# A spectral convolution block in float32: from three merged streams of steps per batch to one fixed period over all batches

## The chip, the cores and the metric

The kernel runs on one core of a Trainium2 chip. The metric is the device time of one execution in microseconds (us), from three runs.

## The reference

The input `x` has 4 batches of 256 x 256 positions with 64 channels, float32. Two layers follow each other. Cut to what is computed:

```python
# layer 0
h  = pw(ln(x, g1, b1), w_te, b_te)                  # 64 -> 128 channels
F  = fft2(h, axes=(1, 2))
fc = gelu(pw(concat(real(F), imag(F)), w_fc, b_fc)) # 256 -> 256
sp = real(ifft2(fc[..., :128] + 1j * fc[..., 128:]))
x1 = x + pw(sp, w_tp, b_tp)                         # 128 -> 64
h2 = pw(ln(x1, g2, b2), w_fe, b_fe)                 # 64 -> 128
d  = gelu(depthwise_conv3x3(h2, w_dw) + b_dw)
x  = x1 + pw(d, w_fp, b_fp)                         # 128 -> 64
# layer 1, along the first image axis, 256 long
trend = moving_average(x, 25)
ys    = einsum('bmnc,cmk->bknc', rfft(x - trend)[:, :128], w_real + 1j * w_imag)
out   = trend + irfft(ys, n=256)
```

## The kernel before

All transforms are matrix products with tables, in float32. Layer 0 is cut into three streams, each a Python generator for one batch that yields after every step.

- `forward_h`, 32 chunks of 8 columns per batch: load `xt`, statistics (`measure`: a square on ScalarE, sums on VectorE), scaling on GpSimd (`norm`), sums of halves on VectorE (`halves`, L341, L343), the transform along the first axis (`transform`, L353, result `ps_y`), copy to `yt`, store to `y_d` in HBM.
- `spectral`, 65 pairs of rows of frequencies per batch, two or three pairs to a group: load `yb`, `transform_w` (L434 with the whole array, L438 and L439 with halves of its columns, result `ps_x`, copied to `xs`), `mix` (L453, halves of its rows, four banks `ps_p`), sums on VectorE (L470), GELU on ScalarE (`activate`, L476), `fold` (L483, one half on VectorE, one on GpSimd), `project` (L508, halves of the columns, `ps_z` copied to `zs`), `turn` (L521, transposes), and once per group `back_w` (L537) with a store to `u_d` in HBM.
- `convolution`, 32 chunks of 8 columns per batch: load `uc` and `x1`; `back_h` (L625, halves of the rows, then three sums on VectorE, L633 and L637); `measure` (square `sq_c`, L294); `norm`; `to_channels` (L657, transposes, copied to `tt`); `row_sums` (L673 to L678); four products of the 3x3 convolution in a form with three row sums per pair of rows: each product is two matmuls with the whole array (`wc_main`, L692) and four with halves of its rows (`wc_half`, L705) into two banks `ps_h`. Products 1 and 2 are `conv_first` (a copy on ScalarE, L724, and four sums on VectorE, L726 and L727), products 0 and 3 `conv_rest` (L733), then `edges` (L745), GELU (`activate`, L750), `finish` in two halves (L756 with halves of the columns, `ps_f` copied to `fs`, L764) and `store` in two halves (transposes L774 of `fs`, sums on VectorE L784, store to `x2_d` in HBM).

So a matmul uses the array as a whole, as two halves of its rows, or as two halves of its columns, and the instructions of one function can be of more than one of these kinds. All results go through one pool of eight PSUM banks. Each bank is reused when the last reader of its former tile is done.

The order of TensorE, VectorE, ScalarE and GpSimd is that in which the Python code issues the instructions (`manual_schedule`); each engine keeps it. SyncE, which issues all DMAs, is ordered by the tile framework. Before, `spaced` gives every step of a generator a place on a common axis, `all_batches` chains the four batches of a stream, and `merge` always advances the stream whose next place is lowest:

```python
at = {
    all_batches(spectral, mixing, 5 * 69, -1.0, -0.08): -1.0,
    all_batches(forward_h, fwd, 4 * 33, -2.05, -1.1): -2.05,
}
...
at[all_batches(convolution, conv, 11 * 36, 0.0, 1.0)] = 0.0
```

The steps of the streams are thus interleaved one by one, by place alone. `convolution` has 36 rounds of 11 steps for 32 chunks: at the start and at the end of each batch its pipeline of five chunks fills and drains. A fourth generator, `matrices`, works out the matrices of layer 1 beside the first batch's `forward_h` (L865, L866, L875). At the end `layer1` (L948) multiplies all batches by them.

Of the kernel before, what the change touches and what calls it, by code (L numbers as in the profile page):

```python
# [2 lines left out]

# [8 lines left out]
F32 = mybir.dt.float32  # L12
# [6 lines left out]
P = 128  # L19
N = 256  # L20
# [88 lines left out]
def conv_seq_kernel(ctx: ExitStack, tc: tile.TileContext, a: dict, tables: bass.AP, out: bass.AP):  # L109
# [7 lines left out]
    spill = ctx.enter_context(tc.tile_pool(name="spill", bufs=2, space=DRAM))  # L117
# [188 lines left out]

    y_ds, u_ds = {}, {}

    def forward_h(b, pool):

        WH = 4
        y_d = spill.tile([P, N, 2, C], F32, tag="y_d", name=f"y_d_{b}")
        y_ds[b] = y_d
# [3 lines left out]
        def load(q):  # L319

            xt = pool.tile([P, 2, 2, WH, C], F32, tag="xt", name=f"xt_{b}_{q}", bufs=3)
            for hf in range(2):
                w0 = hf * P + q * WH
                nc.sync.dma_start(
                    xt[:, :, hf],
                    x[b, :, w0 : w0 + WH, :].rearrange("(t p) w c -> p t w c", p=P),
                )
            chunks[q] = xt

        def measure(q):  # L330
            var[q] = statistics(pool, flat(chunks[q]), f"{b}_{q}")

        def norm(q):
            xt = flat(chunks[q])
            scale(pool, xt, xt, var.pop(q), f"{b}_{q}")

        def halves(q):
            xt = chunks[q]
            xb = pool.tile([P, 2, 2, WH, C], F32, tag="xb", name=f"xb_{b}_{q}", bufs=1)
            for i, op in enumerate((ALU.add, ALU.subtract)):  # L340
                nc.vector.tensor_tensor(xb[:, :, i], xt[:, :, 0], xt[:, :, 1], op)  # L341
            for i, op in enumerate((ALU.add, ALU.subtract)):
                nc.vector.tensor_tensor(xt[:, i], xb[:, 0], xb[:, 1], op)  # L343

        def transform(q):
            n = f"{b}_{q}"
            xt = chunks.pop(q)
            yt = pool.tile([P, 2, WH, 2, C], F32, tag="yt", name=f"yt_{n}")
            for m in range(2):
                ps = bank(f"ps_y_{n}_{m}")  # L350
# [12 lines left out]
            for par in range(2):  # L363
                w0 = par * P + q * WH
                nc.sync.dma_start(y_d[:, w0 : w0 + WH], yt[:, par])

        NCH = P // WH
        load(0)
        for q in range(NCH + 1):
            if q + 1 < NCH:  # L370
                load(q + 1)
            if q < NCH:
                measure(q)
            yield
            if q >= 1:
                halves(q - 1)
            yield
            if q < NCH:
                norm(q)
            yield  # L380
            if q >= 1:
                transform(q - 1)
            yield

    def spectral(b, pool):

        y_d = y_ds.pop(b)
        u_d = spill.tile([P, N, 2, C], F32, tag="u_d", name=f"u_d_{b}")
        u_ds[b] = u_d
        KG, ZS = 4, 1  # L390
        groups, per_group = {}, {}

        def load_group(g):
            n = f"{b}_{g}"
            yb = pool.tile([P, 2, KG, 2 * C], F32, tag="yb", name=f"yb_{n}")
            for t in range(2):
                nc.sync.dma_start(
                    yb[:, t],
                    y_d[g * KG : (g + 1) * KG, t * P : (t + 1) * P].rearrange(
# [3 lines left out]
            groups[g] = yb  # L403

        def begin(g):
            n = f"{b}_{g}"
            yb = groups[g]
            blocks = [(yb, k) for k in range(KG)]
            if g == 0:

                yr = pool.tile([P, 2, 2, 2 * C], F32, tag="yr", name=f"yr_{n}", bufs=1)
# [6 lines left out]
            zt = pool.tile([P, 2, 2, KG, C], F32, tag="zt", name=f"zt_{n}")  # L418
            groups[g] = zt
            per_group[g] = [blocks[i : i + 2] for i in range(0, len(blocks), 2)]  # L420

        def transform_w(pr):
            xs = pool.tile([P, 2, N], F32, tag="xs", name=f"xs_{pr['n']}")
            pr["xs"] = xs
            nb = len(pr["blocks"])
            ps = bank(f"ps_x_{pr['n']}")
            todo = [
# [3 lines left out]
            ]  # L431

            for i, (dst, y, t) in enumerate(todo):
                nc.tensor.matmul(dst, y, cw[:, t, :], start=i == 0, stop=False)  # L434

            for i, (dst, y, t) in enumerate(todo):
# [3 lines left out]
            nc.scalar.copy(xs.rearrange("p j n -> p (j n)")[:, : nb * N], ps[:, : nb * N])  # L440
# [87 lines left out]
        def back_w(g):  # L528
            zt = groups.pop(g)
            ut = pool.tile([P, 2, KG, 2, C], F32, tag="ut", name=f"ut_{b}_{g}")  # L530

            pss = []
            for t in range(2):
                ps = bank(f"ps_u_{b}_{g}_{t}")
# [15 lines left out]
            for wt in range(2):  # L550
                nc.sync.dma_start(
                    u_d[g * KG : (g + 1) * KG, wt * P : (wt + 1) * P].rearrange(
# [5 lines left out]
        prs = []  # L558
        NG = P // KG
        for g in range(NG):  # L560
            slot = 0
            count = KG // 2 + (g == 0)
            for i in range(count):
                prs.append({"g": g, "i": i, "n": f"{b}_{g}_{i}", "special": g == 0 and i == 0})
                prs[-1]["last"] = i == count - 1
                prs[-1]["slot"] = slot
                slot += 1 if prs[-1]["special"] else 2
        load_group(0)
        begin(0)
        for i in range(len(prs) + 4):  # L570
            if i < len(prs):
                pr = prs[i]
                pr["blocks"] = per_group[pr["g"]][pr["i"]]
                transform_w(pr)
                if pr["last"] and pr["g"] + 1 < NG:
                    load_group(pr["g"] + 1)
            if 0 <= i - 2 < len(prs):
                fold(prs[i - 2])
            yield
            if 0 <= i - 4 < len(prs) and prs[i - 4]["last"]:  # L580
                back_w(prs[i - 4]["g"])
            yield
            if 0 <= i - 1 < len(prs):
                mix(prs[i - 1])
            yield
            if 0 <= i - 3 < len(prs):
                turn(prs[i - 3])
            yield
            if 0 <= i - 2 < len(prs):
                project(prs[i - 2])  # L590
            if 0 <= i - 1 < len(prs):
                activate(prs[i - 1])
            if i < len(prs) and prs[i]["last"] and prs[i]["g"] + 1 < NG:
                begin(prs[i]["g"] + 1)
            yield

    def convolution(b, pool):

        u_d = u_ds.pop(b)
# [4 lines left out]
        x1s, ucs, var, xns, ts, ends, stores = {}, {}, {}, {}, {}, {}, {}  # L604
        rows = lambda t: t.rearrange("p t w c -> p (t w) c")

        def load(q):
            n = f"c_{b}_{q}"
            uc = pool.tile([P, W, 2, C], F32, tag="uc", name=f"uc_{n}")
            x1 = pool.tile([P, 2, W, C], F32, tag="x1", name=f"x1_{n}", bufs=6)  # L610
            nc.sync.dma_start(uc, u_d[:, q * W : (q + 1) * W])
# [3 lines left out]
            x1s[q] = x1  # L615
            ucs[q] = uc

        def back_h(q):

            n = f"c_{b}_{q}"  # L620
            uc, x1 = ucs.pop(q), x1s[q]
            pss = [bank(f"ps_s_{n}_{i}") for i in range(2)]
# [16 lines left out]
        def measure(q):  # L639
            var[q] = statistics(pool, rows(x1s[q]), f"c_{b}_{q}")  # L640

        def norm(q):
            n = f"c_{b}_{q}"
            xns[q] = pool.tile([P, 2, W, C], F32, tag="xn", name=f"xn_{n}", bufs=XN)
            scale(pool, rows(x1s[q]), rows(xns[q]), var.pop(q), n)

        tt = pool.tile([P, NP, N + 2], F32, tag="tt", name=f"tt_{b}", bufs=1)
        nc.vector.memset(tt[:, :, 0 : N + 2 : N + 1], 0.0)

        def to_channels(q):  # L650

            xn = xns.pop(q)
            for j in range(0, NP, 2):
                ps = bank(f"ps_t_{b}_{q}_{j}")
# [13 lines left out]
        def row_sums(q):  # L668

            td = pool.tile([P, 4, NP, P], F32, tag="td", name=f"td_{b}_{q}", bufs=TD)  # L670
# [8 lines left out]
            ts[q] = td  # L679

        def beside(q, par):

            got = ((0, q - 1, NP - 1, 1), (1, q, 0, NP - 1)) if par == 0 else (
                (0, q, 1, NP - 1), (NP - 1, q + 1, 0, 1)
            )
            return [(s, ts[k], at, n) for s, k, at, n in got if 0 <= k < NCH]

        def product(q, k):

            pss = [bank(f"ps_h_{b}_{q}_{k}_{par}") for par in range(2)]  # L690
            for par in range(2):
                nc.tensor.matmul(  # L692
                    pss[par],
                    wc_main[:, par, k, :],
                    ts[q][:, k].rearrange("p j i -> p (j i)"),
# [4 lines left out]
            parts = [[(par, *g) for g in beside(q, par)] for par in range(2)]  # L700
            last = [g[-1] for g in parts]
            for g in [g for two in zip_longest(*parts) for g in two if g is not None]:
                par, s, td, at, n = g
                lo = C * (1 - par)
                nc.tensor.matmul(  # L705
                    pss[par][:, s * P : (s + n) * P],
                    wc_half[lo : lo + C, k, :],
# [334 lines left out]
```

## Time and profile before

| | us |
|---|---|
| three runs | 5338.66, 5347.24, 5347.71 (median 5347.24) |
| the profiled execution | 5343.03 |
| its span | 5341.3 |
| TensorE matmul busy | 5162.6 (97%) |
| VectorE busy | 3940.0 (74%) |
| ScalarE busy | 2528.6 (47%) |
| GpSimd busy | 1627.9 (30%) |

Around the span of the profiled execution lie 1.7 us. Busy time of TensorE has the modelled ends of pipelined matmuls in it, so 97% says that a matmul was nearly always under way, not that the array was filled at its best rate. Each float32 matmul is two records in the trace, a transpose one.

The starts of the groups in the trace cut the span into six stages: the first batch's `forward_h` with `matrices` (up to 397 us), `forward_h` and `spectral` (397 to 963), all three streams (963 to 3230), `spectral` and `convolution` (3230 to 4278), `convolution` of the last batch alone (4278 to 4875), and layer 1 (4875 to 5341).

### The profile page before, as it was taken

Reading aid. Unit: us, or ns where it says so; the run is one execution under the profiler, and the core shown is the slowest. Engines: PE = TensorE matmul, PEld = TensorE weight load, DVE = VectorE, ACT = ScalarE, POOL = GpSimd, SP = SyncE. Lnnn points to the kernel's source line nnn. Section 1 sums busy time; section 2 is a strip of 40 time slices with the busy share of each in tenths; the row PEclk is TensorE's granted clock in tenths of the full one; section 3 lists DMA queues with packets and bytes.
Section 4 is the critical chain, followed back from the end, with each engine's and each line's share of the span. In section 5 each row is a group of like instructions: output and inputs, shape, how many; then the busy total and the mean of one; then the engine's idle time right before and its main releaser. Section 6 shows DMA issues by size and latency. Waiting matters only on the chain.

```text
span 5341.3 us, 68749 instructions
## 1 busy us (share of the span) xinstructions
PE 5162.6 (97%) x25435; PEld 2747.3 (51%) x25435; DVE 3940.0 (74%) x6042; ACT 2528.6 (47%) x3678; POOL 1627.9 (30%) x778
## 2 busy tenths in 40 slices
PE   7989999899999999999999999999999999999999
PEld 4445555455555554555555555555555544444444
DVE  6778787887888887987888876777777688883222
ACT  2336676555555554555555544555555433332111
POOL 3444444433333333333333322222221132220000
PEclk9999999999999999999999999999999999999999
DMA  5553343323233323333333222222222422225998
GB/s 171 170 187 115 115 125 100 122 88 111 95 111 115 100 95 117 103 95 102 108 111 113 95 93 75 83 84 83 84 83 79 123 82 93 82 83 170 329 320 283
DMA packets 655157, 653.61 MB, mean 122 GB/s; under 512 B 31373, under 2 KB 506975, under 8 KB 654568
## 3 DMA queue, kind: packets, MB, share of 16 engines
q1 hardware_dynamic: 654824, 649.22, 38.4%
q8 instruction: 203, 3.33, 0.3%
q14 instruction: 130, 1.06, 0.1%
HBM read 363.89 MB, written 285.21 MB: 122 GB/s over the span
## 4 chain that ended last, share of the span: by engine, by line
PE 79%; DVE 10%; issue 5%; DMA 2%; POOL 1%; ACT 1%; SPq 0%; POOLq 0%; DVEq 0%; ACTq 0%
PE ps_h L692 16%; PE ps_h L705 9%; PE ps_u L537 8%; PE ps_o L948 7%; PE ps_p L453 7%; PE ps_x L434 4%; PE ps_f L756 4%; PE ps_z L508 4%; PE ps_x L438 4%; PE ps_y L353 4%; PE ps_s_c L625 4%; PE ps_ft L774 2%; PE ps_zt L521 2%; PE ps_t L657 2%; DVE xt L343 2%
## 5 line engine op out<-in xcount | busy, mean ns | idle before, releaser
L692 PE MATMUL ps_h<-td,wc_main 128*128 128x512 f32 x2048 | 1009.9, 615 | 5.7 <-DVE x_c L633 4.2
L483 POOL TENSOR_TENSOR g<-g 128x512 f32<-128x512 f32 x260 | 358.4, 1379 | 2043.5 <-ACT g L476 2032.3
L470 DVE TENSOR_TENSOR g<-ps_p,g 128x512 f32<-128x512 f32 x1040 | 688.3, 683 | 125.3 <-ACT g L465 106.3
L705 PEld LDWEIGHTS ps_h<-td,wc_half 64*128 64x128 f32 x4032 | 409.3, 186 | 462.4 <-issue 390.8
L304 POOL TENSOR_TENSOR rstd_c<-var_c,minus_half 128x16 f32<-128x16 f32 x128 | 376.8, 2944 | 746.4 <-DVE var_c L298 746.4
L476 ACT ACTIVATE g<-g,b_fc 128x1024 f32<-128x1024 f32 (+1 forms) x520 | 570.4, 1140 | 55.6 <-DVE g L470 55.0
L705 PE MATMUL ps_h<-td,wc_half 64*128 64x128 f32 (+1 forms) x4032 | 583.9, 406 | 2.0 <-DVE td L677 2.0
L692 PEld LDWEIGHTS ps_h<-td,wc_main 128*128 128x128 f32 x2048 | 350.0, 189 | 447.1 <-issue 297.4
L733 DVE TENSOR_TENSOR h<-h,ps_h 128x512 f32<-128x512 f32 x512 | 328.6, 683 | 270.3 <-PE ps_h L705 269.4
L453 PE MATMUL ps_p<-xs,wp 64*128 64x512 f32 (+1 forms) x2080 | 512.8, 605 | 2.0 <-DVE h L733 0.8
L304 POOL TENSOR_TENSOR rstd<-var,minus_half 128x16 f32<-128x16 f32 x128 | 400.2, 3126 | 313.4 <-DVE var L298 255.3
L465 ACT COPY g<-ps_p 128x512 f32<-128x512 f32 (+1 forms) x520 | 295.3, 582 | 413.6 <-PE ps_p L453 410.9
L537 PE MATMUL ps_u<-zt,tab 128*128 128x256 f32 x2048 | 475.2, 385 | 2.3 <-ACT zt L523 1.5
L948 PE MATMUL ps_o<-xc,mt 128*128 128x512 f32 x1024 | 443.4, 595 | 18.6 <-DMA xc<-x_d 18.6
L537 PEld LDWEIGHTS ps_u<-zt,tab 128*128 128x128 f32 x2048 | 378.6, 190 | 89.9 <-issue 15.2
L750 ACT ACTIVATE h<-h,b_conv 128x1024 f32<-128x1024 f32 x256 | 279.9, 1141 | 302.9 <-DVE h L745 302.9
L962 DVE TENSOR_SCALAR oc<-ps_o,b_fp 128x512 f32<-128x512 f32 x128 | 96.1, 750 | 363.7 <-PE ps_o L948 335.9
L948 PEld LDWEIGHTS ps_o<-xc,mt 128*128 128x128 f32 x1024 | 194.4, 191 | 266.8 <-issue 235.7
L434 PEld LDWEIGHTS ps_x<-tab,yb 128*128 128x128 f32 x2032 | 249.7, 193 | 150.6 <-issue 33.7
L508 PE MATMUL ps_z<-g,w_tp 128*64 128x512 f32 x1024 | 281.2, 618 | 39.6 <-DVE g L483 33.1
L353 PE MATMUL ps_y<-xt,tab 128*64 128x512 f32 x1024 | 284.2, 607 | 28.2 <-DVE xt L343 19.0
L453 PEld LDWEIGHTS ps_p<-xs,wp 64*128 64x128 f32 x2080 | 188.2, 186 | 211.6 <-issue 163.9
(131 smaller groups left out, 8374.9 us busy)
## 6 DMA issues: line engine op xcount, KB each, us to landing
xt<-in_x_dram SPq DMA_DIRECT2D x256, 256.0 KB, 3.4
y_d<-yt SPq DMA_DIRECT2D x256, 256.0 KB, 3.3
x_c<-in_x_dram SPq DMA_DIRECT2D x128, 512.0 KB, 5.4
yb<-y_d SPq DMA_DIRECT2D x256, 256.0 KB, 3.3
u_d<-ut SPq DMA_DIRECT2D x256, 256.0 KB, 2.5
uc_c<-u_d SPq DMA_DIRECT2D x128, 512.0 KB, 5.1
x_d<-st SPq DMA_DIRECT2D x128, 512.0 KB, 4.0
xc<-x_d SPq DMA_DIRECT2D x64, 1024.0 KB, 7.8
```

The source lines that it names most:

```text
L304: nc.gpsimd.tensor_tensor(rstd, var, minus_half.to_broadcast([P, n]), ALU.pow)
L353: nc.tensor.matmul(ps[i * C : (i + 1) * C], dh[:, m, i * C : (i + 1) * C], xt[:, i].rearrange("p f w c -> p (f w c)"), start=True, stop=True,)
L434: nc.tensor.matmul(dst, y, cw[:, t, :], start=i == 0, stop=False)
L453: nc.tensor.matmul(ps[:, :nf], wp[rows, cols], rhs[rows], start=True, stop=r == 1 or not pr["special"],)
L470: nc.vector.tensor_tensor(gt[:, i, :nf], re, gt[:, 1, :nf], op)
L476: nc.scalar.activation(g, g, AF.Gelu, bias=b_fc[:, half : half + 1])
L483: eng.tensor_tensor(g[:, 0], g[:, 0], g[:, 1], op)
L508: nc.tensor.matmul(ps[r * C : (r + 1) * C, :nf], w_tp, d[:, :nf], start=True, stop=True)
L537: nc.tensor.matmul(ps[:, r * KG * C : (r + 1) * KG * C], tb[:, t, :], zt[:, t, ri].rearrange("p k c -> p (k c)"), start=ri == 0, stop=ri == 1,
L692: nc.tensor.matmul(pss[par], wc_main[:, par, k, :], ts[q][:, k].rearrange("p j i -> p (j i)"), start=True, stop=False,)
L705: nc.tensor.matmul(pss[par][:, s * P : (s + n) * P], wc_half[lo : lo + C, k, :], td[lo : lo + C, k, at : at + n, :].rearrange("p j i -> p ...
L948: nc.tensor.matmul(ps[:, :nf], mts[i // CM][:, i % CM, t, to * P : (to + 1) * P], xc[:, t, :, :, i, :], start=t == 0, stop=t == 1,)
```

## The change

The generators go. Each stream becomes one set of functions over the chunks of all batches, and `period` calls them in one fixed order for each n. One period takes one chunk of `forward_h`, two pairs of `spectral` and one chunk of `convolution` (in it, five chunks are at different steps, j[0] to j[4]). Where a batch ends the next follows without draining the pipeline. `convolution` starts a batch when `spectral` has stored it, which is the table `chunk_at`. The calls stand so that TensorE's work of a kind comes together: `products` issues the whole-array matmuls of two products, then the half-row matmuls of both; `transform_w` is cut into its whole-array part `xc` and its half-column part `xh`; `conv_rest` does both its products and the edges at once. `spill` gets a third buffer in HBM. Each engine's instructions are the same in number and kind, but for three fewer VectorE rows that set the borders of `tt` to zero; their order changes, and that of the DMAs with it.

```diff
-    spill = ctx.enter_context(tc.tile_pool(name="spill", bufs=2, space=DRAM))
+    spill = ctx.enter_context(tc.tile_pool(name="spill", bufs=3, space=DRAM))
...
-        def product(q, k):
+        def products(j, ks):
...
-            for par in range(2):
+            for (k, par), ps in pss.items():
                 nc.tensor.matmul(
-                    pss[par],
+                    ps,
                     wc_main[:, par, k, :],
...
+            for k in ks:
+                for g in by_turns:
+                    par, s, td, at, n = g
+                    lo = C * (1 - par)
+                    nc.tensor.matmul(
+                        pss[k, par][:, s * P : (s + n) * P],
+                        wc_half[lo : lo + C, k, :],
...
+        def conv_rest(j):
+
+            for r, ms in enumerate(products(j, (0, 3))):
...
+    FWD, KH, COLS = P // 4, P // 2 + 1, N // 8
+    S0 = FWD + 3
+
+    def opened(b):
+
+        return divmod(KH * (b + 1) + 3, 2)
+
+    chunk_at, at = {}, 0
+    for b in range(B):
+        at = max(at, S0 + opened(b)[0] + 1)
+        for q in range(COLS):
+            chunk_at[at] = (b, q)
+            at += 1
+    END = at + 4
+
+    def period(n, f, s, c, m):
+        i = 2 * (n - S0)
+        j = [chunk_at.get(n - k) for k in range(5)] if c else None
...
+        if c:
+            c.to_channels(j[1])
+            c.first(j[3])
+            c.back_h(j[0])
+            if ahead and ahead[1]:
+                c.load(ahead)
+        if s:
+            s.mix(i - 1)
+            s.turn(i - 3)
+            s.back_w(i - 4)
+            s.xc(i)
+        if c:
+            c.measure(j[0])
+        if s:
+            s.xh(i)
+            s.project(i - 2)
+        if c:
+            c.finish(j[4], 0)
+        if on(2):
+            f.transform(n - 2)
+        if on(-1):
+            f.load(n + 1)
+        if m:
+            next(m, None)
+        if s:
+            s.activate(i - 1)
+        if c:
+            c.row_sums(j[1])
+        if s:
+            s.fold(i - 1)
+        if c:
+            c.norm(j[0])
+            c.store(j[4], 0)
+            c.rest(j[3])
+        if s:
+            s.mix(i)
+        if on(0):
+            f.measure(n)
+        if s:
+            s.turn(i - 2)
+            s.back_w(i - 3)
+            s.xc(i + 1)
+            s.xh(i + 1)
+            s.project(i - 1)
+        if c:
+            c.activate(j[3])
+            c.finish(j[4], 2)
+        if s:
+            s.activate(i)
+        if on(1):
+            f.halves(n - 1)
+        if s:
+            s.fold(i)
+        if on(0):
+            f.norm(n)
+        if m:
+            next(m, None)
+        if c:
+            c.store(j[4], 2)
+            if ahead and not ahead[1]:
+                c.load(ahead)
...
-            at = {
-                all_batches(spectral, mixing, 5 * 69, -1.0, -0.08): -1.0,
-                all_batches(forward_h, fwd, 4 * 33, -2.05, -1.1): -2.05,
-            }
...
+                for n in range(S0):
+                    period(n, f, None, None, m)
+                s.load(0)
+                s.begin(0)
...
+            for n in range(S0, S0 + opened(B - 1)[0] + 1):
+                period(n, f, s, c, None)
...
-            merge(at, float(B + 1))
+            for n in range(S0 + opened(B - 1)[0] + 1, END):
+                period(n, None, None, c, None)
```

With 4 batches S0 is 35. Periods 0 to 34 hold `forward_h` and `matrices`, 35 to 69 `forward_h` and `spectral`, 70 to 129 all three streams, 130 to 166 `spectral` and `convolution`, 167 to 202 `convolution` alone.

## The prediction

> **What bounds the kernel now.** I read the page first, then the busy time by stage, then the timeline of single chunks.
>
> ```profile
> span 5341.3 us, 68749 instructions
> PE 5162.6 (97%) x25435; PEld 2747.3 (51%) x25435; DVE 3940.0 (74%) x6042; ACT 2528.6 (47%) x3678; POOL 1627.9 (30%) x778
> ```
>
> TensorE is the bound, but 97% is busy, not work. A record of 512 columns follows the last one after 0.43 us (shown below), 0.83 ns a column; two half-array records go side by side. Summed over all groups that makes 4485 us. The remaining 857 us are what a reordering can reach.
>
> ```profile
> 25.00:397.00 372.00, 339.92 (x1127) 175.89 (x1125) 277.28 (x352) 116.73 (x174) 170.00 (x70) 0.98 0.55 174
> 397.00:963.00 566.00, 538.28 (x3292) 314.88 (x3290) 448.74 (x628) 386.52 (x575) 248.29 (x125) 0.99 0.39 118
> 963.00:3230.00 2267.00, 2215.71 (x11809) 1200.64 (x11810) 1877.29 (x2892) 1195.48 (x1741) 809.95 (x384) 0.99 0.32 103
> 3230.00:4278.00 1048.00, 1039.32 (x5632) 579.77 (x5634) 749.06 (x1193) 533.77 (x774) 245.13 (x129) 1.00 0.28 87
> 4278.00:4875.00 597.00, 581.74 (x2545) 279.49 (x2542) 479.40 (x803) 208.19 (x288) 153.83 (x64) 0.99 0.23 79
> ```
>
> Columns: stage, its length, busy time of TensorE, weight loads, VectorE, ScalarE, GpSimd, then granted clock and DMA. These are stages 1 to 5; 6 is layer 1, 466 us, unchanged. VectorE is busy 79 to 83% of stages 2, 3 and 5: a faster TensorE would soon meet it.
>
> Now one chunk of the last batch alone (stage 5), and a place where two lines of the same array kind meet:
>
> ```profile
> 4501.09 1.06 ACT L294 ACTIVATE sq_c<-x_c 128x1024 f32<-128x1024 f32 x1 [1.62 <-DVE x_c L637]
> ...
> 4501.26 1.98 PE L692 MATMUL ps_h<-td,wc_main 128*128 128x512 f32 x4
> ...
> 4502.05 1.11 ACT L724 COPY h<-ps_h 128x512 f32<-128x512 f32 x2
> ...
> 4503.18 1.14 PE L705 MATMUL ps_h<-td,wc_half 64*128 64x128 f32 x8
> ...
> 4504.42 0.69 DVE L726 TENSOR_TENSOR h<-h,ps_h 128x512 f32<-128x512 f32 x1 [0.55 <-PE ps_h L705]
> ...
> 4505.27 1.08 PE L756 MATMUL ps_f<-h,w_fp 128*64 128x512 f32 x4
> ...
> 4506.27 1.98 PE L692 MATMUL ps_h<-td,wc_main 128*128 128x512 f32 x4
> 4506.42 0.58 ACT L764 COPY fs<-ps_f 128x512 f32<-128x512 f32 x1 [0.35 <-PE ps_f L756]
> ```
> ```profile
> 2510.90 0.19 PEld L625 LDWEIGHTS ps_s_c<-uc_c,tab 64*128 64x128 f32 x2 [0.24 <-issue]
> 2511.33 0.19 PEld L453 LDWEIGHTS ps_p<-xs,wp 64*128 64x128 f32 x2 [0.23 <-issue]
> 2511.76 1.88 PE L453 MATMUL ps_p<-xs,wp 64*128 64x512 f32 x8
> ```
>
> From L692 (whole array) to L705 (half rows): 4503.18 - 4501.26 = 1.92 us for four records that need 4 x 0.43 = 1.71, so 0.21 lost. From L756 (half columns) to L692: 1.00 against 2 x 0.43, 0.14 lost. From L625 to L453, both half rows, the step stays 0.43: nothing lost. So it is the change of array kind that costs. Over the trace the median is 0.16 to 0.21 for each pair of kinds; I take 0.2. The old instruction order has 2914 changes, 583 us; waits and the ends make up the other 270.
>
> **What the change removes.** In the new order there are 1270 changes, 1644 fewer: 329 us on the busiest engine. By stage: 65, 212, 473, 301 and 216, where before there were 65, 365, 1334, 677 and 470. A three-stream period has 8. Its TensorE work at full pace is 29.9 us (row products 10.2, `mix` 3.4, `back_w` 3.4, `xc` and `xh` 3.4, `back_h`, `project`, `finish` and `transform` 1.7 each, transposes 2.6), with 8 x 0.2 it is 31.5. Before, stage 3 took 2267 / 64 = 35.4 a chunk.
>
> [...]
>
> **What it adds: waits in the order of ScalarE.** Before, a step of another kind lay between each `finish` and its `store`: above, L764 starts 0.15 us into L692 and TensorE goes on. In the new TensorE order `store` (transposes of `fs`) follows at once, or after one more group, and TensorE can do nothing until ScalarE has copied `fs`. What stands ahead of that copy on ScalarE decides. ScalarE keeps its order: above, L724's product was there at about 4501.33 (its L705 started at 4500.19 and takes 1.14), and the copy starts at 4502.05, behind the square of L294.
>
> [...]
>
> Stage 5, `convolution` alone, one period from the start of `to_channels`:
> - `to_channels` 8 x 0.107 = 0.86; eight records L692 3.41 and a change 0.2; the first product's half rows 0.85; the second's reach VectorE 1.24 after their start (4503.18 to 4504.42): 6.56.
> - VectorE: four sums L726, L727 2.73, three sums of `back_h` 2.7 until ScalarE can start (4516.44 to 4519.14 for the next chunk): 11.99. The square `sq_c` 1.06 stands ahead of `fs` on ScalarE; `fs` 0.58: 13.65. TensorE has finished L756 at 9.0 and waits 4.6.
> - `store` 0.43, `conv_rest`: L692 3.41, change 0.2, first product in half rows, to VectorE 1.24: 18.95. Two sums each of products 0 and 3, 1.27 and then 1.41 to the GELU: 21.65. TensorE has done its second `finish` at 20.5.
> - GELU 2.19, ahead of the second `fs`, 0.58: 24.4, `store` 0.43: 24.9.
>
> That is a chain through one period with no cover: `measure`, `norm` and `row_sums` lie inside it. Before, the steady pace here was (4677 - 4532) / 8 = 18.1 a chunk. 32 full periods at 24.9 are 797; the four that drain, without `back_h` and then with less, 19.4 + 18.5 + 18.5 + 4 = 60. Stage 5: 857 after 597, a loss of 260.
>
> Stages 3 and 4. The first `fs` is covered by `transform` in stage 3 (in stage 4 it costs 0.7). The second isn't. The order on ScalarE is `zs` of `project`, two GELUs of `activate(j[3])`, `fs`; on TensorE `project`, `finish`, `store`. `project` ends at 30.0 of the period (its last result 0.17 later, a record takes 0.6), then 0.07, 0.58, 2.19, 0.58 and 0.06: `store` at 33.65, `finish` done at 30.85. With the 0.43 of the transposes the period is 34.1, 2.6 over TensorE's own. The GELUs themselves wait for nothing: their sums (`edges`) end at about 27. The queue on VectorE behind the late `store`: its two sums end 3 to 4 us into the next period, the next product comes at 6.56. Banks: eight, reused in the order freed; the tightest are `z` and `f`, which take those of `mix` or `back_h`, freed 1 to 4 us before. In stage 4 without `transform` it is 33.1, and 33.7 where `back_w` stands in the second half and the last bank of `mix` waits 0.6 for the sums of the first `store`; 33 of 37 periods are so: 33.6. The batches' pipelines no longer drain, but the first fills: 44 us less in stage 3 (14.6 + 13 + 13 + 3), 15 less at the free period 134.
> Stage 3: 60 x 34.1 - 44 = 2002 (2267 before). Stage 4: 37 x 33.6 - 15 = 1228 (1048). Together 85 less, mostly because 12 rounds of filling and draining are gone.
>
> Stage 2, `forward_h` and `spectral`. TensorE's work 14.5 and 6 changes, 15.7; VectorE's 15.1; ScalarE's 13.2. `mix` waits for `xs`, which on ScalarE stands behind two copies of the last `mix`, the square and `zt`, and those behind the GELU of the pair before, which waits for nothing earlier than the copies `yt`. `project` waits 0.9 for its bank. Followed through, this closes at 17.5. Between 16 (VectorE nearly full) and 18.2 (the pace before): 17.5, since two engines near the limit seldom do better. 35 x 17.5 - 10 = 602 (566).
>
> Stage 1. Rounds of 10.6 before, in which `transform` waits about 2 us for L343 of the same round; now `halves` are a period ahead. TensorE needs 8.9, VectorE 8.4 with L343 at 3.0 beside GpSimd. Between 9.0 and 10.6 I take 9.8: 340, and 10 for the first load of `y_d`, 350 (372).
>
> DMAs: the loads `uc`, `x1`, `xt`, `yb` stay a period ahead of use (3.4 to 5.4 us to landing against 17 to 34), and the third buffer of `spill` frees the stores. At nothing; if a batch's first `uc` came late, some 5 us each, 20 in all.
>
> **Sum.** 25 + 350 + 602 + 2002 + 1228 + 857 + 466 = 5530. Stage 4 before took 1048 where work (901) and changes (135) make 1036, 0.4 a chunk that no row explains; 97 periods of stages 3 and 4 at 0.4 are 39. With 1.7 around the span: 5571, against 5343.03 of the profiled execution, 0.1% under the median 5347.24. Bounds: stage 1 -28 to +28, 2 -50 to +25, 3 and 4 -60 to +70, 5 -30 to +30.
>
> **Rivals.**
> 1. Faster: the copies of `fs` don't hold TensorE, because ScalarE reaches them before TensorE is done. Then stage 5 stays at 18.1 (32 x 6.8 = 218 less) and stages 3 and 4 lose 2.6 x 97 = 252: 5101. It decides from half of that on: at a stage 5 of 21 us and a wait of 1.4 in stages 3 and 4 the kernels are equal. For it: ScalarE is idle half the time. Against: the chain is in its order, and each link has a row. 0.10.
> 2. Much slower: VectorE becomes the bound in stage 3. It was busy 1877 / 64 = 29.3 a chunk; L343 takes 3.00 for two beside GpSimd, 1.29 without. If sums that now wait in lumps add 2 us to each of the 97 periods: 5571 + 194 = 5765. 0.12.
> 3. The change does not do what it says: the 0.2 is latency that comes back in the larger groups. 13 changes a period saved come back, 2.6 x 97 = 252: 5823. The step of 0.43 from L625 to L453 speaks against it. 0.05.
>
> **How the numbers follow.** The forecast has 0.71, and its own bounds, two of them at a time, 5450 to 5690. Between it and rival 1 lies 0.02 for no change (0.2% is about what a measurement of this kernel can tell). The range 5400 to 5720 leaves out rival 1 and most of rivals 2 and 3. Slower 0.71 + 0.12 + 0.05 = 0.88, faster 0.10.
>
> **What would show it.** Right: in stage 5, chunks 24 to 25 us apart, and `ps_ft` waiting for `fs` of ScalarE at the top of the waits, some 8 us a chunk; TensorE busy about two thirds there; in stage 3 one wait of 2 to 3 us a period at the same place, and periods of 34. Wrong: chunks 18 us apart at the end, or periods under 32 in stage 3. If TensorE's first wait there is for VectorE, rival 2 holds; if L692 and L705 keep their old steps in groups twice as long, rival 3.

## The result, and the profile after

The changed kernel takes 5723.1 us (median of 4 runs, 5720.38 to 5726.7), the kernel before 5345.73 (median of 4, 5338.66 to 5347.71): a ratio of 1.0709 [1.069, 1.0727], 377 us slower. The forecast was 228 us slower, and its range ended 3 us under the measured time. The profiled execution took 5720.38 us.

The page of the changed kernel, its span, its engines and its row of the granted clock:

```profile
span 5718.4 us, 69126 instructions
...
PE 5056.7 (88%) x25435; PEld 2904.5 (51%) x25435; DVE 3831.0 (67%) x6039; ACT 2525.6 (44%) x3678; POOL 1672.6 (29%) x778
...
PEclk9989999999999999999999999999997787778999
```

TensorE issues the same 25435 records as before and has less busy time (5162.6 before), but 88% of the span where it had 97%: it waits. The clock row shows where to look: 7 and 8 in the seven slices ahead of layer 1, and an 8 in the first stage. Busy time by stage (stage, length, busy time of TensorE, weight loads, VectorE, ScalarE, GpSimd, granted clock, DMA share, GB/s):

```profile
25.00:456.00 431.00, 352.94 (x1039) 181.39 (x1037) 221.85 (x347) 109.75 (x165) 178.44 (x69) 0.89 0.45 145
456.00:1012.00 556.00, 539.18 (x3522) 337.91 (x3522) 466.10 (x681) 401.86 (x611) 264.03 (x137) 0.99 0.43 129
1012.00:3016.00 2004.00, 1859.96 (x10777) 1112.42 (x10776) 1688.78 (x2646) 1101.06 (x1597) 782.10 (x359) 0.99 0.36 108
3016.00:4256.00 1240.00, 1123.66 (x6322) 680.74 (x6321) 844.23 (x1342) 600.98 (x870) 281.61 (x145) 0.98 0.25 75
4256.00:5249.00 993.00, 729.34 (x2745) 393.61 (x2743) 501.87 (x853) 222.66 (x310) 165.72 (x64) 0.80 0.19 60
5249.00:5719.00 470.00, 447.11 (x1028) 196.06 (x1026) 97.00 (x130) 87.97 (x128) 0.00 (x0) 0.99 1.00 308
```

| stage | before | forecast | after | after less forecast |
|---|---|---|---|---|
| 1, `forward_h` and `matrices` | 372 | 350 | 431 | +81 |
| 2, `forward_h` and `spectral` | 566 | 602 | 556 | -46 |
| 3 and 4, three streams, then two | 3315 | 3269 | 3244 | -25 |
| 5, `convolution` alone | 597 | 857 | 993 | +136 |
| 6, layer 1 | 466 | 466 | 469.4 | +3.4 |

The last column adds up to +149.4, which is 5720.4 less 5571. Apart from 3.4 us in layer 1, two stages are slower than before, the first and the fifth, and in both only one of the three streams runs.

The waits of the changed kernel, rows of `store` (engine, line, waited for: us in total, times, longest us):

```profile
PEld ps_ft_c L765 <- ACT fs_c L754: 688.9, 200, 5.5
...
PE ps_ft_c L765 <- ACT fs_c L754: 511.3, 200, 4.7
```

These are one wait seen twice, by the weight loads and by the matmuls of the same transposes. It is TensorE's first wait, as forecast, while `ps_ft` waiting for `fs` came to 13.5 us in 8 waits of the weight loads before (5.7 by the matmuls). The timeline shows its cause, first in stage 3, then in stage 5 (start, us, instruction, in brackets the idle time before it and what ended it):

```profile
2029.56 1.03 PE L746 MATMUL ps_f_c<-h_c,w_fp 128*64 128x512 f32 x4
...
2029.86 0.59 ACT L517 COPY zs<-ps_z 128x512 f32<-128x512 f32 x1 [0.35 <-PE ps_z L513]
...
2030.34 2.19 ACT L740 ACTIVATE h_c<-h_c,b_conv 128x1024 f32<-128x1024 f32 x2
2032.43 0.57 ACT L754 COPY fs_c<-ps_f_c 128x512 f32<-128x512 f32 x1
...
2033.06 0.66 PE L765 MATMUL ps_ft_c<-ident,fs_c 128*128 128x128 f32 x4 [2.47 <-ACT fs_c L754]
```

ScalarE takes up `fs` only after `zs` and the two GELUs, 1.84 us after L746 has ended. The transposes behind it still run at full pace, four in 0.66; in this period the clock record falls to 0.50 only at 2034.2.

```profile
4958.33 1.08 PE L746 MATMUL ps_f_c<-h_c,w_fp 128*64 128x512 f32 x4
...
4962.12 1.06 ACT L295 ACTIVATE sq_c<-x_c 128x1024 f32<-128x1024 f32 x1 [5.15 <-DVE x_c L623]
4963.09 0.57 ACT L754 COPY fs_c<-ps_f_c 128x512 f32<-128x512 f32 x1
...
4963.71 1.12 PE L765 MATMUL ps_ft_c<-ident,fs_c 128*128 128x128 f32 x4 [4.30 <-ACT fs_c L754]
...
4964.62 6.11 PE L680 MATMUL ps_h_c<-td_c,wc_main 128*128 128x512 f32 x8
...
4974.42 2.19 ACT L740 ACTIVATE h_c<-h_c,b_conv 128x1024 f32<-128x1024 f32 x2 [10.77 <-DVE h_c L735]
4976.52 0.56 ACT L754 COPY fs_c<-ps_f_c 128x512 f32<-128x512 f32 x1
...
4977.13 1.12 PE L765 MATMUL ps_ft_c<-ident,fs_c 128*128 128x128 f32 x4 [3.47 <-ACT fs_c L754]
...
4978.04 1.91 PE L642 MATMUL ps_t_c<-ident,xn_c 128*128 128x128 f32 x8
4979.75 3.67 PE L680 MATMUL ps_h_c<-td_c,wc_main 128*128 128x512 f32 x8
```

The first `fs` stands behind the square `sq_c`, which waits 5.15 us for VectorE's sums, the second behind the GELU, which waits 10.77. TensorE stands still for 4.30 and 3.47 us. And behind each wait it is slow: eight records L680 take 6.11 us where the next eight take 3.67, four L765 1.12 against 0.66 in stage 3. It is the same work, in part at half the clock: the trace's record of the granted clock has 0.50 from 4962.82 to 4969.65 us and from 4976.48 to 4979.89 us, and 1.00 between and after; 0.80 is the mean of the stage.

### The profile page after: what moved, and what is told of

The parts are those of the page before. It is cut to its first block, busy times and chain, and to the rows that moved or that the text cites. A ratio compares the mean times of both kernels' runs of the same rounds, so it can differ in the third digit from the quotient of the medians.

```text
span 5718.4 us, 69126 instructions
## 1 busy us (share of the span) xinstructions
PE 5056.7 (88%) x25435; PEld 2904.5 (51%) x25435; DVE 3831.0 (67%) x6039; ACT 2525.6 (44%) x3678; POOL 1672.6 (29%) x778
## 4 chain that ended last, share of the span: by engine, by line
PE 80%; ACT 9%; DVE 5%; issue 4%; DMA 1%; SPq 0%; ACTq 0%; POOL 0%; DVEq 0%; POOLq 0%
PE ps_h_c L680 17%; PE ps_h_c L695 8%; PE ps_u L547 8%; PE ps_p L458 7%; PE ps_o L890 7%; PE ps_y L356 5%; ACT h_c L740 4%; PE ps_s_c L611 4%; PE ps_x L438 4%; PE ps_ft_c L765 3%; PE ps_x L431 3%; PE ps_z L513 3%; PE ps_t_c L642 3%; PE ps_zt L526 2%; PE ps_f_c L746 2%
## 5 line engine op out<-in xcount | busy, mean ns | idle before, releaser
L680 PE MATMUL ps_h_c<-td_c,wc_main 128*128 128x512 f32 x2048 | 1028.6, 649 | 0.0
L475 DVE TENSOR_TENSOR g<-ps_p,g 128x512 f32<-128x512 f32 x1040 | 687.8, 682 | 53.3 <-ACT g L470 35.3
L765 PE MATMUL ps_ft_c<-ident,fs_c 128*128 128x128 f32 x1024 | 202.9, 330 | 511.3 <-ACT fs_c L754 511.3
L680 PEld LDWEIGHTS ps_h_c<-td_c,wc_main 128*128 128x128 f32 x2048 | 418.6, 216 | 434.7 <-issue 410.7
L717 DVE TENSOR_TENSOR h_c<-h_c,ps_h_c 128x512 f32<-128x512 f32 x256 | 175.3, 685 | 586.2 <-PE ps_h_c L695 566.2
L695 PEld LDWEIGHTS ps_h_c<-td_c,wc_half 64*128 64x128 f32 x4032 | 416.7, 187 | 238.5 <-issue 194.1
L695 PE MATMUL ps_h_c<-td_c,wc_half 64*128 64x128 f32 (+1 forms) x4032 | 513.3, 392 | 0.0
L765 PEld LDWEIGHTS ps_ft_c<-ident,fs_c 128*128 128x128 f32 x1024 | 129.7, 163 | 734.4 <-ACT fs_c L754 688.9
L740 ACT ACTIVATE h_c<-h_c,b_conv 128x1024 f32<-128x1024 f32 x256 | 279.9, 1143 | 355.2 <-DVE h_c L735 355.2
L725 DVE TENSOR_TENSOR h_c<-h_c,ps_h_c 128x512 f32<-128x512 f32 x512 | 316.6, 679 | 165.9 <-PE ps_h_c L695 165.9
L488 DVE TENSOR_TENSOR g<-g 128x512 f32<-128x512 f32 x260 | 204.0, 785 | 287.2 <-ACT g L481 283.8
L356 PE MATMUL ps_y<-xt,tab 128*64 128x512 f32 x1024 | 300.9, 663 | 72.6 <-issue 72.2
L775 DVE TENSOR_TENSOR st<-x_c,ps_ft_c 128x256 f32<-128x256 f32 x512 | 262.0, 589 | 139.5 <-PE ps_ft_c L765 139.5
```

Of the source, the lines that this page charges most:

```text
L356: nc.tensor.matmul(ps[i * C : (i + 1) * C], dh[:, m, i * C : (i + 1) * C], xt[:, i].rearrange("p f w c -> p (f w c)"), start=True, stop=True,)
L475: nc.vector.tensor_tensor(gt[:, i, :nf], re, gt[:, 1, :nf], op)
L488: eng.tensor_tensor(g[:, 0], g[:, 0], g[:, 1], op)
L680: nc.tensor.matmul(ps, wc_main[:, par, k, :], ts[j][:, k].rearrange("p j i -> p (j i)"), start=True, stop=False,)
L695: nc.tensor.matmul(pss[k, par][:, s * P : (s + n) * P], wc_half[lo : lo + C, k, :], td[lo : lo + C, k, at : at + n, :].rearrange("p j i -> ...
L740: nc.scalar.activation(flat, flat, AF.Gelu, bias=b_conv)
```

## The experiments

All but b4 change the new kernel. e1 to e4 and b3 are single runs, the first four set against the new kernel's median of 5723.1; the kernel before, run beside the experiments, had medians of 5343.1 (e1 to e4), 5345.22 (b1 to b4) and 5345.89 (c1). Steady paces from the traces, in us (a period of stage 2 is 16.2 in every kernel made from the new one; of before and b4, the means of stages 3 and 4 are given):

| kernel | time | stage 1, a round | stage 3, a period | stage 4 | stage 5, a chunk |
|---|---|---|---|---|---|
| before | 5345.73 | 10.6 | 35.4 | 32.8 | 18.1 |
| after | 5723.1 | 13.2, each fourth 11.6 | 34.1 | 34.0 | 28.7 and 29.3 in turn |
| e1 | 5372.79 | 13.2, each fourth 11.6 | 32.3 | 32.2 | 23.9 |
| e2 | 5597.96 | 13.2, each fourth 11.6 | 34.1 | 34.0 | 26.2 and 25.0 |
| e3 | 5597.0 | 9.0 | 34.1 | 34.0 | 28.7 and 29.3 |
| e4 | 5577.97 | 13.2, each fourth 11.6 | 34.1 | 34.0 | 24.4 |
| b1 | 5133.3 | 9.0 | 32.3 | 32.2 | 20.1 to 23.3 |
| b2 | 5195.56 | 9.0 | 33.1 | 32.6 | 20.5 |
| b3 | 5218.6 | 9.0 | 32.3 | 32.2 | 20.1, some 21.5 |
| b4 | 5316.52 | 10.6 | 35.3 | 32.0 | 18.1 |
| c1 | 5034.14 | 9.0 | 32.3 | 32.2 | 17.3 |

**e1: the second `finish` ahead of the GELU.** The theory says that what stands ahead of `fs` on ScalarE is what TensorE waits for; the rival was VectorE.

```diff
-            c.activate(j[3])
             c.finish(j[4], 2)
+            c.activate(j[3])
```

> The changed kernel with the second finish called ahead of activate, so that on ScalarE the copy fs stands ahead of the two GELUs of the convolution; TensorE's order stays. Theory (TensorE waits for a copy that stands behind the GELUs): periods of the three-stream stage fall from 34.1 to about 31.7 us, the next stage's as much, and in the last batch alone the second wait falls from 3.9 to about 0.9 with some half-clock time: 144 + 85 + 150 less, about 5345 us. Rival (VectorE, busy 84% in the three-stream stage, sets the period): less than 50 us gained.

5372.79 us, 350 less; 5345 us was expected, with periods of 31.7 in stage 3, which came to 32.3. Two calls change places and nothing else. The timeline of e1 in stage 3:

```profile
2017.41 0.58 ACT L754 COPY fs_c<-ps_f_c 128x512 f32<-128x512 f32 x1 [0.19 <-PE ps_f_c L746]
2017.90 2.19 ACT L740 ACTIVATE h_c<-h_c,b_conv 128x1024 f32<-128x1024 f32 x2
2018.05 0.66 PE L765 MATMUL ps_ft_c<-ident,fs_c 128*128 128x128 f32 x4 [0.69 <-ACT fs_c L754]
```

The wait is 0.69 where it was 2.47, and the period is shorter by 1.8, the same amount. VectorE does not step in: the rival falls.

**e2: the first `finish` ahead of the square.**

```diff
+            c.finish(j[4], 0)
             c.measure(j[0])
...
-            c.finish(j[4], 0)
```

> The changed kernel with the first finish called ahead of measure, so that on ScalarE its copy fs stands ahead of the square sq_c. Theory: only the stage of the last batch alone gains: the first wait of 4.6 us becomes about 0.8, and the matmuls after it run at full clock again, 2.4 to 2.9 us: periods from 28.9 to about 22.3, 230 us less in 34 periods, and up to 0.7 a period in the stage before it (26 us): about 5470 us. Rival (the period of that stage is set by VectorE or by loads): no change.

5597.96 us, 125 less, half of what was expected. The timeline of e2 in stage 5:

```profile
4702.88 1.11 PE L765 MATMUL ps_ft_c<-ident,fs_c 128*128 128x128 f32 x4 [6.21 <-ACT fs_c L754]
...
4714.65 0.66 PE L765 MATMUL ps_ft_c<-ident,fs_c 128*128 128x128 f32 x4 [0.74 <-ACT fs_c L754]
...
4725.19 2.19 ACT L740 ACTIVATE h_c<-h_c,b_conv 128x1024 f32<-128x1024 f32 x2 [7.49 <-DVE h_c L735]
```

The first wait is gone, 0.74 for 4.30. The second grew from 3.47 to 6.21: its GELU waits for VectorE's `edges`, and VectorE, which has the sums of `back_h`, `measure`, `row_sums` and `conv_rest` in a row, came no earlier for TensorE being early. So in stage 5 the removed wait turned for the most part into the other one: the two together fell by 0.8 us. The pace fell by 3.4; the larger part of it, 2.5, is the clock, which no longer drops behind the first wait: eight L680 there take 3.60 us for 6.11, and the granted clock of the stage is 0.87 for 0.80.

**e3: `matrices` at the end of the period.** Stage 1 was the surprise, so its timeline in the changed kernel comes first:

```profile
298.49 2.49 PE L356 MATMUL ps_y<-xt,tab 128*64 128x512 f32 x8 [2.00 <-issue]
...
304.65 0.69 DVE L845 TENSOR_TENSOR mt<-t,ps_m 128x512 f32<-128x512 f32 x1 [5.07 <-PE ps_m L837]
305.26 1.21 DVE L296 TENSOR_REDUCE total<-xt 128x16 f32<-128x1024 f32 x1
...
309.27 1.29 DVE L343 TENSOR_TENSOR xt<-xb 128x512 f32<-128x512 f32 x2
310.06 4.09 PE L356 MATMUL ps_y<-xt,tab 128*64 128x512 f32 x8 [2.00 <-issue]
314.08 1.13 PE L827 MATMUL ps_v<-t,w 128*128 128x512 f32 x2
```

`mt` (L845) of the first `next(m)` stands ahead of `measure` and `halves` on VectorE and waits 5.07 us for TensorE's product of this very period. `measure` and `halves` follow it, and the next `transform` (L356) follows `halves`. That closes a loop: L356, products of `matrices`, `mt`, `measure`, `halves`, L356. With both `next(m)` at the end, `mt` stands behind `halves`.

```diff
             if on(-1):
                 f.load(n + 1)
-            if m:
-                next(m, None)
...
             if m:
+                next(m, None)
                 next(m, None)
```

> The changed kernel with both steps of matrices at the end of the period in place of one in the middle. Theory (in the first stage a loop runs from transform over the matrices' product, its sum mt on VectorE, measure and halves back to the next transform, and TensorE's clock halves in the wait): rounds fall from 13.2 and 11.6 us to 9 to 10, 90 to 120 us less, about 5615 us. Rival (the loads of xt or GpSimd's norm set the round): no change, 5720.

5597.0 us, 126 less, 120 of it in the first stage. A stage and a line of e3, by windows and by timeline:

```profile
25.00:336.00 311.00, 295.28 (x1038) 162.37 (x1037) 224.40 (x348) 110.70 (x166) 178.25 (x69) 0.99 0.61 200
```

```profile
257.31 1.94 PE L356 MATMUL ps_y<-xt,tab 128*64 128x512 f32 x8
```

311 us for 431, the clock 0.99 for 0.89. A round is 9.0, which is what the prediction gave as TensorE's own need (8.9). Without the wait L356 takes 1.94; behind it 2.49 to 4.09. The loop alone costs 2.6 us a round (11.6 for 9.0, the clock record at 1.00); in a round of 13.2 the clock is at 0.50 for 3.41 us (from 310.46 on in the rows above), which makes it 1.6 us longer.

**e4: matmuls in the waits of stage 5.** If what a chunk of stage 5 takes beyond the forecast's chain is the half clock, then keeping TensorE busy in the waits must shorten the time, with more work. The added products are read by nobody.

```diff
+    def keep_busy(n, at, count):
+        ps = bank(f"ps_k_{n}_{at}")
+        for k in range(count):
+            nc.tensor.matmul(
+                ps, ident, tab[:, 0:512], start=k == 0, stop=k == count - 1
+            )
...
+            if not s:
+                keep_busy(n, 0, 4)
             c.store(j[4], 0)
...
+            if not s:
+                keep_busy(n, 2, 3)
             c.store(j[4], 2)
```

> The changed kernel with matmuls whose result nobody reads (four of 512 columns before the first store, three before the second) in the two waits of the stage of the last batch alone. Theory (on top of the waits TensorE's granted clock falls to half after them): with more work the stage gets shorter, periods from 28.9 to about 25 us, the granted clock there from 0.80 to near 1: about 5590 us. Rival (the 4 us over the chain worked out before are something else): no change, or some 1 to 3 us a period more.

5577.97 us, 145 less, near the 5590 expected. Stage 5 of e4, by windows, and one chunk of its timeline:

```profile
4256.00:5100.00 844.00, 798.16 (x3221) 391.53 (x3220) 501.79 (x849) 217.13 (x306) 165.74 (x64) 1.00 0.22 71
```

```profile
4949.97 3.70 PE L937 MATMUL ps_k<-tab,ident 128*128 128x512 f32 x8
...
4954.35 0.66 PE L765 MATMUL ps_ft_c<-ident,fs_c 128*128 128x128 f32 x4 [0.67 <-ACT fs_c L754]
4954.84 3.60 PE L680 MATMUL ps_h_c<-td_c,wc_main 128*128 128x512 f32 x8
```

The chunks come every 24.4 us; the forecast's chain said 24.9. The chain of dependences is the same as in the changed kernel and the clock differs, 1.00 for 0.80. For the chunk shown above the difference closes from the rows: eight L680 start to next 3.53 against 6.03, two groups L765 0.46 each, L642 1.04 against 1.91, together 4.3, and 24.4 + 4.3 = 28.7.

**b1: the three moves together.** e1, e2 and e3 in one kernel.

> The three moves of order together: second finish ahead of activate, first finish ahead of measure, both steps of matrices at the end of the period. Theory (the changed kernel lost its gain to copies held back on ScalarE, to the half clock after those waits and to the loop in the first stage): first stage 336 us, three-stream periods 32.3, the next stage 32.2, chunks of the last batch about 18 as VectorE's sums then fill them: 5723 - 126 - 97 x 1.8 - 34 x 10.7 = about 5060 us, 5.4% under the kernel before. Rival (the waits move to another place when one is taken away): 5150 to 5300 us.

5133.3 us, ratio to before 0.9606 [0.9592, 0.962]. So the grouped order with its copies in time is faster than before; the expected 5060 was missed in stage 5, where chunks of 20.1 to 23.3 came in place of 18; the rival's 5150 to 5300 was not reached either. A wait for another engine appears there, as the rival said, in the timeline of b1:

```profile
4612.39 1.90 POOL L306 TENSOR_TENSOR xn_c<-x_c,rstd_c 128x1024 f32<-128x1024 f32 x1
4614.35 1.09 PE L642 MATMUL ps_t_c<-ident,xn_c 128*128 128x128 f32 x8 [1.72 <-POOL xn_c L306]
```

`to_channels` stands at the start of the period, before GpSimd has finished `norm` of the same chunk.

**c1: b1 with `to_channels` later in stage 5.**

```diff
         if c:
-            c.to_channels(j[1])
+            if s:
+                c.to_channels(j[1])
...
         if c:
+            if not s:
+                c.to_channels(j[1])
             c.row_sums(j[1])
```

> The three moves, and in periods without spectral to_channels stands ahead of row_sums and the first store instead of at the start of the period. Theory (with the three moves the last batch's 20 to 21 us per chunk are TensorE waiting 1.7 us for GpSimd's xn at the start of the period, 0.7 twice for fs, and some half clock after it): the wait for xn and the first wait for fs go, chunks 17.3 to 18 us apart, 36 x 2.8 = 100 us less than with the three moves alone, about 5030 us. Rival (VectorE's sums set that stage): 19 us or more a chunk, 5080 us or more.

5034.14 us, ratio to before 0.942 [0.9404, 0.9435], the fastest of all. The page of c1 and its stage 5:

```profile
span 5028.8 us, 69124 instructions
...
PE 4831.5 (96%) x25435; PEld 2782.1 (55%) x25435; DVE 3813.1 (76%) x6039; ACT 2515.5 (50%) x3678; POOL 1674.6 (33%) x778
```

```profile
4000.00:4500.00 500.00, 478.21 (x2292) 253.86 (x2290) 422.43 (x725) 187.38 (x259) 150.18 (x58) 1.00 0.27 89
```

Chunks of 17.3, the clock at 1.00. Four moves of calls lie between 5723 and 5034; the work is the same.

**b2: what the changes of array kind are worth.** b1, with each product by itself again: four changes more in a period, 512 more in all.

```diff
-            m1s, m2s = products(j, (1, 2))
+            (m1s,), (m2s,) = products(j, (1,)), products(j, (2,))
...
-            for r, ms in enumerate(products(j, (0, 3))):
+            for r, ms in enumerate(products(j, (k,))[0] for k in (0, 3)):
```

> The three moves, but with the four products one at a time, each with its whole-array and then its half-row matmuls, as before the change: 512 more changes of array kind (1781 in all). Theory (a change of kind costs 0.2 us where TensorE is the bound): 97 periods x 4 x 0.2 = 78 us more than the kernel with the three moves alone, up to 102 if the last batch pays too. Rival (the 0.2 is latency that a finer order hides, and VectorE gets its first product earlier): within 20 us of it, or less time.

5195.56 us, ratio 0.9722 [0.9706, 0.9738]; 62 us over b1, where 78 were expected. Stage 3 went from 32.3 to 33.1: 0.8 for four changes, 0.2 each, the prediction's price; TensorE's idle time in it stayed the same (34 and 33 us in 1600). In stage 4 it is 0.1 each, since a wait became shorter by the rest: `ps_p` for its bank, 13.8 us in 950 us of b1, 3.8 in b2. In stage 5, where TensorE waits for others, the pace is 20.5, within b1's spread.

**b3: batches that drain.** b1, with four empty periods between batches, 11 more in all, since one was empty in b1 too.

```diff
+        at += 4
-    END = at + 4
+    END = at
```

> The three moves, but four periods are left free between the convolution's batches, so that its pipeline drains and fills at each batch as before the change. Theory (TensorE's work is the same, and a free period is a short one): chunks move from 32 us beside spectral to 18 alone, with a poorer cover in the periods that fill and drain: 20 to 60 us more than the kernel with the three moves. Rival (the continuous streams are the main gain): 12 periods of 18 to 32 us more, 200 us and over.

5218.6 us, 85 over b1. Batches that follow without draining are worth that much, more than the theory's 20 to 60 and far from the rival's 200. In the traces b3 is 100 us shorter than b1 up to the end of `spectral` (3850 us for 3950), and the convolution alone after it takes 898 us for 718; its chunks there are 20.1 and more, not the 18 of the theory.

**b4: the kernel before with grouped products.** Only the products are taken two at a time, in the old merged order.

```diff
-        def product(q, k):
+        def products(q, ks):
...
-            for par, m1 in enumerate(product(q, 1)):
+            m1s, m2s = products(q, (1, 2))
+            for par, m1 in enumerate(m1s):
...
-                conv_rest(q - 3, 0)
+                conv_rest(q - 3)
...
-                conv_rest(q - 3, 1)
```

> The kernel before the change with its merged generators, but with two products issued together (products 1 and 2, then 0 and 3 and the edges in one step): 477 changes of kind fewer (2437 in place of 2914) and nothing else of the change. Theory: 477 x 0.2 = 95 us less, about 5250 us, less what the larger lumps give back in waits. Rival (in the old order the price of a change is hidden): within 0.3% of 5345 us, or slower.

5316.52 us, ratio 0.9949 [0.9934, 0.9963], 29 less where 95 were expected. Counted in the two traces there are 476 changes fewer, 0.06 us each. By stage (cut at the last `store` of a batch): in stage 4 there are 116 fewer and it is 22 us shorter, 0.19 each; in stage 3 231 fewer and 5 us; in stage 5 128 fewer and 1 us, the pace stays 18.1. TensorE's busy time falls in the other two stages as well, by 32 us in stage 3 and 22 in stage 5, but its idle time grows there from 51 to 79 us and from 15 to 37. A row of the waits of b4:

```profile
PE ps_ft L780 <- ACT fs L770: 33.4, 46, 0.7
```

Before, the same wait was 5.7 us in 8 times. With `conv_rest` in one step, nothing of it stands any more between the second `finish` and its `store`, so b4 has the changed kernel's wait for `fs`, 25 of the 33.4 us in stage 5. So the changes were saved in all three stages, and in stages 3 and 5 the waits took the gain, although TensorE was 97% busy before.

## Why the prediction was right or wrong

**Direction and mechanism held.** The path "`finish`, copy of `fs` behind other work on ScalarE, `store`" was forecast, is TensorE's first wait, and falls from 2.47 to 0.69 us in stage 3 when the calls that stand ahead are moved (e1: 350 us from a swap of two lines). The period of stage 3 was forecast as 34.1 and is 34.1, of stage 4 as 33.6 and is 34.0. Stages 3 and 4 together came 25 us under their 3269, because the allowance of 39 us for what no row explained was too much; it should have been 14. Most of the 14 is found: in seven periods of about 35.5 us the wait of 2.4 to 2.5 us for `fs` left TensorE at half clock (the record at 0.50 for 3.41 us), 1.4 us each, 10 in all.

**Stage 5, +136: the term that was mis-sized is "24.9".** The chain was right, e4 has 24.4. A chunk measured 28.7 and 29.3 in turn, 29.0 on the mean: 32 x 4.1 = 131 of the 136. The step that failed is that it took every duration from before, where TensorE seldom waits long (the granted clock was 0.99 in this stage), and so at full clock. With the waits of 4.30 and 3.47 us the clock record goes to 0.50, for 6.83 and 3.41 us in the chunk shown above, which adds 4.3 us to one chunk and 4.9 to the next over the 24.4 of e4. The forecast has no term for this: the granted clock in its rows of stages 1 to 5 was 0.98 to 1.00.

**Stage 1, +81: the step that failed is "now `halves` are a period ahead".** Rounds of 13.2 and 11.6 came in place of 9.8. The quoted words are so in the order of the calls for one chunk, but `mt` of the first `next(m)` stands ahead of them on VectorE and waits for TensorE in the same period. I followed `fs` through ScalarE's order and did not follow `mt` through VectorE's. The range of -28 to +28 was drawn from 9.0 and 10.6, and a new loop was outside both. e3 shows the 9.0 that the lower end assumed.

**Stage 2, -46: the term "17.5" was too large.** A period takes 16.2, 0.5 over TensorE's own 15.7. That "two engines near the limit seldom do better" was no step worked out from rows, and it failed: VectorE is busy 466 of 556 us and costs almost nothing.

The errors of stages 2 and of 3 with 4 hid 71 us of those of 1 and 5.

**The price of a change of kind, 0.2,** shows in full where no wait makes up for it (stage 3 of b2, stage 4 of b4), and by half or not at all where one does (stage 4 of b2, stages 3 and 5 of b4). The claim "329 us on the busiest engine" is thus an upper bound: the three-stream period is near the 31.5 of work and changes once `fs` is in time (32.3 in e1), while stage 5 came under its old pace only with the calls moved (17.3 in c1 against 18.1).

**The rivals.** The first, that the copies do not hold TensorE, was wrong for this kernel and is what b1 and c1 make true: it gave 5101, b1 has 5133 and c1 5034. The second, VectorE as the bound of stage 3, is refuted: 32.3 in e1. The third, that the 0.2 is latency that comes back in larger groups, is refuted by b2, and in stages 3 and 5 of the old order (b4) the gain did come back, but as waits for other engines and not in the groups.

**What stays open.** What each of the waits that grew in stage 3 of b4 comes from, and how the 180 us that b3 adds at its end divide among its drained periods and its slower chunks.

## What to carry to other kernels

When work of one kind is grouped on one engine, the steps that lay between a producer and the transfer of its result vanish as cover: for every eviction count what stands ahead of it in the order of the engine that does it, and put the eviction first. Follow that for each stage and each engine, also where fewer streams run, since there the same order has no cover. And price a long wait of TensorE twice, once for itself and once for the slower clock of the work behind it: here the waits of 4.30 and 3.47 us brought 4.3 to 4.9 us a chunk of such work with them.

## What the runs showed of the hardware

More work made the kernel faster: e4 adds seven matmuls of 512 columns to each chunk of stage 5, none of them read, and saves 145 us.

In the changed kernel the length of a wait alone does not say whether the clock falls. Counted over the transposes of each `store`: after waits of about 2.5 us the clock record was at 0.50 within the next 3.4 us in 13 of 88 cases; after waits of 3 us and more in 67 of 68, three times only when the transposes were done. The one of the 68 that cost nothing was 3.46 us long, ahead of 4282.12, with the record at 1.00. In the first stage, with the same 2.00 us ahead of it, L356 takes 2.49, 4.09, 3.95 and 3.53 us in a turn of four rounds (51.2 us together), and the 11.6-us round is the one that begins with 2.49, the only one of the four at full clock (1.00 from 298.49 to 310.06, 0.87 in each of the other three).

The clock record goes with the two kinds of chunk in stage 5 of the changed kernel as well. Over two chunks, 58.0 us from 4963.71 on, the granted clock is 0.79. Around the end of their four waits, 4.30, 3.47, 4.30 and 3.46 us long, the record is at 0.50 for 6.83, 3.41, 6.83 and 6.83 us, and the eight L680 behind them take 6.11, 3.67, 5.42 and 5.03 us.
